# Attention's output weights multiplied into the joining weights beside the first scan; the joining product reads attention's result itself

## The chip, the cores and the metric

The kernel is one program on one core of a Trainium2 chip, in fp32 throughout. The metric is the device time of one execution in microseconds (us), and the number that counts is the median of several. A core has five engines that run their own instruction streams and meet through semaphores: TensorE (PE, matrix products; its weight loads are shown apart as PEld), VectorE (DVE), ScalarE (ACT), GpSimd (POOL) and SyncE (SP, which here issues DMA transfers).

## The reference, cut to what matters

A block of two layers over 4 images of 256 channels and 32x32 = 1024 positions. The first layer mixes channels and positions, the second is a mixture of 8 experts, two for each position.

```
x = x + metaformer(layer_norm_c(x))          # below
t = tokens(x);  t = t + experts(layer_norm(t))

def metaformer(x):                           # B=4, N=1024, C=256
    xm = four state-space scans of 64 channels (128 inner, 16 states) + skip * xn
    Q  = sigmoid(conv1d(conv1d(xm)))         # gate
    R  = conv1d(conv1d(gate * xm)) + gate * xm
    xm2 = conv1d(conv1d(cat[xs, R])) + xs
    x_local  = depthwise conv1d(xm2)
    x_global = mha(xm2)                      # 8 heads; ends in  o @ outw.T + outb
    x_out = concat[x_local, x_global] @ fc_w.T + fc_b
    xi = gelu(layernorm(x_out))
    xi = depthwise 3x3 conv(ln_hw(xi))
    return layernorm(xi) @ proj_w.T + proj_b
```

Attention's last step, `o @ outw.T + outb`, is followed by nothing but the joining product: `x_global` is the second half of what `fc_w` is multiplied with. So `x_global @ fc_g.T` equals `o @ (fc_g @ outw).T + fc_g @ outb`, with `fc_g` the half of `fc_w` that belongs to it.

## The kernel before

The data lie with channels on the 128 partitions (two chunks of 128) and positions along the free axis, mostly in halves of 512. A product of the first layer (`product`, L393) is a row of 128x512 matmuls that accumulate in one tile of PSUM: one for each chunk of 128 input channels. `in_turn` (L414) makes a list of such products and lets an ACT or DVE instruction take each result out two products later.

The order of all engines' instructions is written by hand, in Python, while the program is built. Work is given as generators; each `yield k` says that its next piece comes k ticks later. `beat` (L1475) is one tick: it lets all running generators that are due emit their next piece, in the order in which they were started. Engines then run their instructions in the order in which they were emitted, so a piece that is emitted a tick earlier stands earlier in its engine's queue, and no time is fixed.

The spine is the scan (L1521 to L1556): image b is scanned in 8 parts (4 groups of channels by 2 halves of the positions) of 16 steps. After each step (`scan`, L804) comes one beat. A step takes `decay` on ACT (L686, exp), `inflow` on DVE (L695, `dBu`), the scan instruction itself on DVE (L710, `hs`), a multiply on POOL (L718) and now and then matmuls on PE: `bs` (L681, inputs spread over states), `yp` (L728, sums over states). At fixed steps of a part the projections of the next group (`up`, `zp`, `dtp`), its silu and its softplus are emitted. SP issues the spreads of dt and c over the partitions (`dts` L652, `cs` L675), and `xd` and `XL` transfers.

Beside the scan of image b runs the rest of image b−1: `convolutions` in the first half, then, after a point at which everything running is finished, `attention` (L1069) followed by `joined` (L1216), and beside these `local`, `around` (L1258; depthwise 3x3 taps on DVE) and `sent_off` (L1301) of image b−2, which waits for a flag: `joining` of image b−1, or for the last scan `attending`. The last image's own `attention`, `joined`, `around` and `sent_off` run when the scans are over, beside the expert tiles (`tiles`, L1354): for each tile 8 `h` matmul groups (L2235), gelu on ACT (L2240, `hs`), `y` products (L2248), with the next tile's rows transposed on PE (L2194) and copied by DVE (L2198, `xT`). In this tail `pace` (L1168) sets how many ticks lie between two pieces of a tile: 2 during the joining products, 1.1 during normalisation, 0.67 during the taps.

`joined(b)` does, in this order:

- four products `ao` with the output weights `aoutT_s`, two matmuls each, on attention's result `oT` (two tiles, the former `qk` buffers); ACT takes each out as `xglo` with the bias `ob` (L1227). In ticks: a piece each 2 ticks for images 0 and 2 (10 ticks in all), each tick for images 1 and 3 (6 ticks).
- for image 2 only, it waits until image 1's `sent_off` has set `projected`.
- four products `fc` with `fcT_s`, four matmuls each: chunks 0 and 1 on `xloc`, chunks 2 and 3 on `xglo`; ACT takes each out as `xc` with the bias `fcb`.
- it sets `joining`, normalises over channels (`inverse_deviation`, L1173: squares on ACT, `var` matmuls, then `root`, L387, a logarithm and an exponential on ACT as `r`, L390 and L391, and two DVE multiplies) and applies gelu on ACT.

`sent_off(b)` takes a mean by PE (`mean`, L409), subtracts it on DVE (`xi`), finds a second deviation (`fin`), makes four products `pr` with `projT_s`, and ends with the experts' routing (`dispatch`).

`later_weights` (L209) runs once, from part 1 of image 0: the list `later` holds six weights that `load` put there (`aoutT_s` first), issued on SP at one each four ticks; then follow small preparations: `obp` (L245, the bias `ob` of attention's output from the values' bias), `prp` (L257), and the centring of `fcT_s` and of its bias `fcb` (L271 to L287), so that the mean over channels that the norm after the joining product would subtract is already zero.

Of the kernel before, what the change touches and what calls it, by code (L numbers as in the profile page):

```python
# [10 lines left out]
AF = mybir.ActivationFunctionType  # L11
ALU = mybir.AluOpType
AX = mybir.AxisListType

P = 128
C = 256
NC2 = C // P
# [58 lines left out]
def network(  # L76
# [27 lines left out]
    nc = tc.nc  # L104
    shifted = sums is None
    B = x.shape[0]
# [4 lines left out]
    def ps_tile(name):  # L111

        return psum.tile([P, HALF], F32, tag="ps", name=name)
# [9 lines left out]
    def col(name, i=0, rows=slice(0, P)):  # L123
        at = _AT[name] + i
        return V[rows, at : at + 1]

    ident = cpool.tile([P, P], F32, name="ident")
# [20 lines left out]
    with tc.tile_pool(name="w_conv", bufs=1) as wp, tc.tile_pool(  # L148
# [22 lines left out]
        def load(ap, name, eng=None):  # L171
            t = wp.tile(list(ap.shape), F32, name=name)
            if eng is None:
                later.append((t, ap))
            else:
                eng.dma_start(t, ap)
            return t
# [8 lines left out]
        nc.scalar.dma_start(inzT_s, inwT[:, :, DIN : 2 * DIN])  # L186
        xpwT_s = load(xpwT, "xpwT_s", nc.scalar)
        moutT_s = load(moutT, "moutT_s", nc.gpsimd)
        aoutT_s = load(aoutT, "aoutT_s")
        projT_s = load(projT, "projT_s")  # L190
        fcT_s = load(fcT, "fcT_s")

# [11 lines left out]
        ob = wp.tile([P, NC2], F32, name="ob")  # L204
        prb = wp.tile([P, NC2], F32, name="prb")
        fcm = wp.tile([P, 2 * NC2, 1], F32, name="fcm")
        fcb = wp.tile([P, NC2], F32, name="fcb")

        def later_weights():  # L209

            nc.sync.dma_start(vb, vbias.rearrange("a (c p) -> p (a c)", p=P))
            for t in (qdwT_s, qpwT_s, qdw_b):
                nc.gpsimd.memset(t, 0.0)
            yield 1
            nc.sync.dma_start(
                qdwT_s[:, 0 : NC2 * 3 * NB], qdwT.rearrange("p c k n -> p (c k n)")
            )
            yield 1
            for i in range(4):
                nc.sync.dma_start(qpwT_s[32 * i : 32 * i + NB, :], qpwT)  # L220
                if i % 2 == 0:
                    at = _AT["qdw_b"]
                    nc.sync.dma_start(qdw_b[32 * i : 32 * i + NB, :], vecs[0:NB, at : at + 1])
                yield 1
            for t, ap in later:
                nc.sync.dma_start(t, ap)
                yield 4
            for ci in range(NC2):
                nc.sync.dma_start(
                    wqkT_s[:, ci].rearrange("p w (i x) -> p (w i) x", x=2 * HD)  # L230
                    .rearrange("p c (i x) -> p c i x", x=HD),
                    wqkT[:, ci].rearrange("p c (i x) -> p c i x", x=2 * HD)[:, :, :, 0:HD],
                )
                yield 4
            for i in range(4):
                at = _AT["qk_b"] + i // 2
                nc.sync.dma_start(
                    qk_b[ts(i, HD), :], vecs[ds(64 * (i % 2), HD), at : at + 8 : 2]
                )
                yield 1  # L240

            obp = ps_tile("obp")
            for co in range(NC2):
                for ci in range(NC2):
                    nc.tensor.matmul(  # L245
                        obp[:, co : co + 1], aoutT_s[:, ci, ts(co, P)], vb[:, ci : ci + 1],
                        start=(ci == 0), stop=(ci == NC2 - 1),
                    )
            yield 1
            nc.vector.tensor_tensor(  # L250
                ob, obp[:, 0:NC2], V[:, _AT["attn_outb"] : _AT["attn_outb"] + NC2], ALU.add
            )

            prp = ps_tile("prp")
            for co in range(NC2):
                for ci in range(NC2):
                    nc.tensor.matmul(  # L257
                        prp[:, co : co + 1], projT_s[:, ci, ts(co, P)], col("norm_b", ci),
                        start=(ci == 0), stop=(ci == NC2 - 1),
                    )  # L260
            yield 1
            nc.vector.tensor_tensor(
                prb, prp[:, 0:NC2], V[:, _AT["proj_b"] : _AT["proj_b"] + NC2], ALU.add
            )
            for ci in range(NC2):
                nc.vector.tensor_scalar(
                    projT_s[:, ci, :], projT_s[:, ci, :], col("norm_w", ci), None, ALU.mult
                )
            yield 1

            nc.vector.tensor_reduce(fcm, fcT_s, AX.X, ALU.add)  # L271
            yield 1
            nc.vector.tensor_scalar(fcm, fcm, 1.0 / C, None, ALU.mult)
            nc.vector.tensor_tensor(
                fcT_s, fcT_s, fcm.to_broadcast([P, 2 * NC2, C]), ALU.subtract
            )
            fbp = ps_tile("fbp")
            for c in range(NC2):
                nc.tensor.matmul(
                    fbp[:, 0:1], ones_mean, col("fc_b", c), start=(c == 0), stop=(c == NC2 - 1)  # L280
                )
            yield 1
            nc.vector.tensor_tensor(
                fcb, V[:, _AT["fc_b"] : _AT["fc_b"] + NC2], fbp[:, 0:1].to_broadcast([P, NC2]),
                ALU.subtract,
            )

        ones = experts.every
# [73 lines left out]
        def a8(name):  # L362
            return act8.tile([P, NC2, N], F32, tag="a8", name=name)
# [10 lines left out]
        def a2(name, rows=P):  # L374
            return act2.tile([rows, HALF], F32, tag="a2", name=name)

        def half(h):
            return ts(h, HALF)
# [14 lines left out]
        def product(name, w, co, chunks, kept=None, at=0):  # L393

            out = ps(name)
            if kept is not None:
                nc.tensor.matmul(out, ident, kept, start=True, stop=False)
            for ci, chunk in enumerate(chunks):
                nc.tensor.matmul(
                    out, w[:, at + ci, ts(co, P)], chunk, start=(ci == 0 and kept is None),  # L400
                    stop=(ci == len(chunks) - 1),
                )
            return out
# [10 lines left out]
        def in_turn(items, make, use, lag=2, every=1):  # L414

            made, lag = [], lag // every
            for at in range(len(items) + lag):
                if at >= lag:
                    use(items[at - lag], made[at - lag])
                if at < len(items):  # L420
                    made.append(make(items[at]))
                yield every

        CO_H = [(co, h) for co in range(NC2) for h in range(2)]
# [791 lines left out]
        def joined(b):  # L1216

            xloc, oT = XLOC.pop(b), OT.pop(b)
            pace(b, PACE["product"])
            xglo = a8(f"xglo_{b}")  # L1220
            T["attending", b] = True
            yield from in_turn(
                CO_H, lambda at: product(
                    f"ao_{b}_{at[0]}_{at[1]}", aoutT_s, at[0],
                    [oT[ci][:, half(at[1])] for ci in range(NC2)],
                ),
                lambda at, r: nc.scalar.activation(  # L1227
                    xglo[:, at[0], half(at[1])], r, AF.Identity, bias=ob[:, at[0] : at[0] + 1]
                ), every=2 if b in (0, B - 2) else 1,
            )  # L1230

            while b == B - 2 and not T.get(("projected", b - 1)):
                yield 1
            xc = XC[b] = a8(f"xc_{b}")
            both = (xloc, xglo)
            yield from in_turn(
                CO_H, lambda at: product(
                    f"fc_{b}_{at[0]}_{at[1]}", fcT_s, at[0],
                    [both[ci // 2][:, ci % 2, half(at[1])] for ci in range(4)],
                ),  # L1240
                lambda at, r: nc.scalar.activation(
                    xc[:, at[0], half(at[1])], r, AF.Identity, bias=fcb[:, at[0] : at[0] + 1]
                ), lag=(4, 4, 2, 2)[b], every=(4, 2, 2, 1)[b],
            )

            T["joining", b] = True
            pace(b, PACE["norm"])
            yield from inverse_deviation(f"lgn_{b}", xc, b == B - 1)
            for c in range(NC2):
                nc.scalar.activation(  # L1250
                    xc[:, c, :], xc[:, c, :], AF.Gelu, bias=col("lgn_b", c), scale=col("lgn_w", c)
                )
            loaded[0] = None
            if b < B - 1:
                log_exp()
            yield 2
# [259 lines left out]
        with tc.manual_schedule(engines=ALL):  # L1516
# [4 lines left out]
            for b in range(B):  # L1521
                for p in range(PARTS):
                    at = b * PARTS + p
                    stop = b > 0 and p == PARTS // 2 - 1 or at == len(parts) - 1
# [883 lines left out]
```

## Time and profile before

| | us |
|---|---|
| runs | 2222.41, 2226.15, 2234.33 |
| median | 2226.15 |
| the profiled execution | 2211.61 |
| its span (first to last instruction) | 2209.9 |
| mean TensorE clock granted, of full | 0.953 |
| first and last `ao` matmul start | 548.2, 1721.1 |
| first and last scan instruction on DVE start | 55.5, 1461.9 |

The profile is of one execution, a little faster than the runs. All durations in the text come from it. In a row of a table of groups stand the line, the engine, the operation, what it writes and reads with the sizes, and how often; after the first bar the busy time and the mean of one instruction, after the second the idle time of the engine just ahead of these instructions and what ended it. Releasers are inferred from semaphores; where an instruction waits for two things, the later one is named. An fp32 matmul appears as two records, so 16 products of two matmuls are 64 records. Ends of matmuls are modelled and overlap the next one's start, so a matmul's cost in a full PE queue is read from the distance between starts.

### The profile page before, as it was taken

The numbers are of one execution on the slowest core, as the hardware profiler recorded it, in microseconds if no ns is written. First come the engines' busy times: TensorE is split into PE (matmuls) and PEld (weight loads), VectorE is DVE, ScalarE is ACT, GpSimd is POOL, SyncE is SP. The second block draws the span as 40 slices with busy tenths as digits, with TensorE's granted clock in tenths as the row PEclk, the third lists the DMA queues.
The fourth block names the chain that finished last, engine by engine and source line by source line (L and its number), as shares of the span: only waits on it lengthen the run. The fifth ranks groups of instructions, "written<-read, shape, count | busy, mean of one in ns | idle before, by whom it ended". The sixth has DMA issues, their size and how long they took to land. (4 is left out here: it accounts for less than half of the span.)

```text
span 2209.9 us, 28348 instructions
## 1 busy us (share of the span) xinstructions
PE 1971.1 (89%) x8766; PEld 881.5 (40%) x8766; DVE 1532.8 (69%) x2231; ACT 1230.8 (56%) x2302; POOL 1047.0 (47%) x930
## 2 busy tenths in 40 slices
PE   6877878999988999987889999778999999999995
PEld 2112112322212332322123223225643678888884
DVE  3989998858998978898898877985365265221211
ACT  4665657678777667775656766624167433222221
POOL 0787887712888730675985025752140022422221
PEclk8898999999999999998999999889999999999997
DMA  3665553401544421243643033344230166966655
GB/s 94 146 161 129 125 126 87 111 15 63 121 120 103 104 49 39 69 108 89 168 102 92 1 91 83 104 153 143 87 103 1 46 203 176 265 182 191 177 157 165
DMA packets 157090, 251.44 MB, mean 114 GB/s; under 512 B 34740, under 2 KB 101332, under 8 KB 156664
## 3 DMA queue, kind: packets, MB, share of 16 engines
q1 hardware_dynamic: 136560, 223.47, 37.1%
q0 software_dynamic: 12720, 17.32, 3.9%
q10 hardware_dynamic: 7640, 8.65, 1.2%
q8 instruction: 74, 1.21, 0.2%
q14 instruction: 96, 0.79, 0.1%
HBM read 137.22 MB, written 36.62 MB: 79 GB/s over the span
## 5 line engine op out<-in xcount | busy, mean ns | idle before, releaser
L718 POOL TENSOR_TENSOR dA<-hs,cs 128x512 f32<-128x512 f32 x512 | 680.2, 1338 | 388.6 <-DVE hs L710 312.9
L689 ACT ACTIVATE dA<-dts,A 128x512 f32<-128x512 f32 x512 | 359.0, 718 | 160.2 <-DMA dts<-dt 83.4
L2275 POOL DMA_INDIRECT Y<-ys,dest x68 | 109.1, 1605 | 515.7 <-DVE ys L2267 509.0
L728 PE MATMUL yp<-dA,quads 128*32 128x512 f32 x1024 | 261.6, 639 | 62.2 <-POOL dA L718 49.3
L1098 ACT ACTIVATE e<-st 128x512 f32<-128x512 f32 x512 | 263.8, 604 | 95.1 <-PE st L1088 85.0
L699 DVE TENSOR_TENSOR dBu<-dts,bs 128x512 f32<-128x512 f32 x384 | 260.2, 678 | 53.9 <-PE bs L681 13.0
L2240 ACT ACTIVATE hs<-h,b 128x256 f32<-128x256 f32 (+1 forms) x256 | 110.6, 477 | 332.8 <-PE h L2235 230.6
L2248 PE MATMUL y<-w,hs 128*128 128x256 f32 (+1 forms) x1088 | 243.6, 382 | 2.5 <-ACT hs L2240 2.5
L710 DVE TENSOR_TENSOR_SCAN hs<-dA,last,dBu 128x512 f32<-128x512 f32 x192 | 243.7, 1269 | 1.8 <-POOL xm L921 1.4
L2235 PE MATMUL h<-xT,w 128*128 128x256 f32 (+1 forms) x1024 | 238.3, 389 | 4.0 <-DVE xT L2198 4.0
L710 DVE TENSOR_TENSOR_SCAN hs<-dA,dBu 128x512 f32<-128x512 f32 x192 | 232.0, 1209 | 10.2 <-PE av L1108 5.1
L1144 DVE TENSOR_TENSOR e<-e,e 128x512 f32<-128x512 f32 x256 | 170.0, 725 | 75.6 <-ACT e L1098 39.5
L2235 PEld LDWEIGHTS h<-xT,w 128*128 128x128 f32 x1024 | 194.9, 191 | 49.6 <-issue 12.0
L2248 PEld LDWEIGHTS y<-w,hs 128*128 128x128 f32 (+1 forms) x1088 | 197.0, 188 | 39.4 <-issue 8.9
L681 PE MATMUL bs<-u,xpwT_s 128*32 128x512 f32 x1024 | 160.2, 657 | 40.4 <-DVE hs L710 16.3
L2198 DVE COPY xT<-xp 128x512 f32<-128x512 f32 (+1 forms) x36 | 23.2, 645 | 236.1 <-PE xp L2194 235.8
L1088 PE MATMUL st<-qk 32*128 32x512 f32 x1024 | 175.7, 640 | 1.9 <-DVE hs L710 1.9
L728 PEld LDWEIGHTS yp<-dA,quads 128*32 128x32 f32 x1024 | 48.3, 114 | 253.9 <-POOL dA L718 152.7
L1134 PE MATMUL av<-e,v 128*32 128x512 f32 x1024 | 139.5, 608 | 0.0
L1088 PEld LDWEIGHTS st<-qk 32*128 32x128 f32 x1024 | 60.1, 183 | 116.8 <-issue 86.2
L1108 PE MATMUL av<-e,every 128*32 128x512 f32 x512 | 87.6, 601 | 3.9 <-DVE e L1144 3.9
L699 DVE TENSOR_TENSOR bs<-dts,bs 128x512 f32<-128x512 f32 x128 | 86.2, 674 | 2.1 <-DMA dts<-dt 2.1
(330 smaller groups left out, 2716.5 us busy)
## 6 DMA issues: line engine op xcount, KB each, us to landing
dts<-dt SPq DMA_DIRECT2D x512, 128.0 KB, 2.4
w<-in_W_dram SPq DMA_DIRECT2D x124, 512.0 KB, 4.2
cs<-cd SPq DMA_DIRECT2D x512, 64.0 KB, 2.1
xs<-XS SPq DMA_DIRECT2D x32, 260.0 KB, 3.7
xd<-xn SPq DMA_DIRECT2D x64, 128.0 KB, 2.9
xn<-in_x_dram SPq DMA_DIRECT2D x8, 512.0 KB
XL<-xl SPq DMA_DIRECT2D x8, 512.0 KB
xl<-XL SPq DMA_DIRECT2D x4, 1024.0 KB
```

Source lines behind the costliest of these rows:

```text
L681: nc.tensor.matmul(bs[r], xpwT_s[:, n, s : s + 1].to_broadcast([P, 32]), T[b, n, "u"][:, half(h)], start=True, stop=True,)
L689: nc.scalar.activation(dA, T[b, n, h, "dts", g][:, 0, :], AF.Exp, scale=A[:, g, n, q : q + 1])
L699: nc.vector.tensor_tensor(dBu, T[b, n, h, "dts", g][:, 1, :], T[b, n, h, "bs", q], ALU.mult)
L710: nc.vector.tensor_tensor_scan(hs, T[b, n, h, "dA", i], dBu, 0.0 if h == 0 else last, ALU.mult, ALU.add)
L718: nc.gpsimd.tensor_tensor(dA, hs, T[b, n, h, "cs", q], ALU.mult)
L728: nc.tensor.matmul(T[b, n, h, "yp"][ts(g, 32)], quads, T[b, n, h, "dA", q * GD + g], start=False, stop=(q == GS - 1),)
L1088: nc.tensor.matmul(sts[i], k[r, ts(kt, P)], q[r, half(h)], start=True, stop=not shifted)
L1098: nc.scalar.activation(es[i], sts[i], AF.Exp, scale=1.0 / HD**0.5)
L1134: nc.tensor.matmul(accs[0][ts(i, HD)], v8[:, kt, ts(4 * g + i, HD)], es[i], start=(kt == 0), stop=(kt == NK - 1),)
L1144: nc.vector.tensor_tensor(first[i], first[i], es[i], ALU.add)
L2235: nc.tensor.matmul(hp[:, i, :], w1(c, k0 + i), xT[:, c, :], start=(c == 0), stop=(c == NC2 - 1))
L2248: nc.tensor.matmul(yp[ts(k % parts, n), ts(t % 2, C)], hidden(k)[:, ds(t * P, n)], w2(k), start=(k < parts), stop=(k >= NHC - parts),)
```

## The change

The diff does three things.

1. `aoutT_s` is no longer one of the lasting weights. It leaves the list `later` and is loaded at the end of `later_weights` into a short-lived buffer, four ticks before its use. With the list one shorter and these four ticks added, the rest of `later_weights` stands where it stood; one `yield 1` is new at its end.
2. Four transposes turn `aoutT_s` round on PE, ACT copies the result to `aout`; four matmuls of 256 columns (`joint`) multiply it with the centred half of `fcT_s` that belongs to attention, and four of one column (`fob`) multiply that half with `ob`. DVE adds `fob` to `fcb`; ACT writes `joint` over that half of `fcT_s`.
3. `joined` loses the four `ao` products, their ACT evictions, the buffer `xglo` and their ticks; the `fc` products read `oT` in place of `xglo`, with as many matmuls as before.

The flag `attending` is set at the same place, just ahead of where `ao` stood. With the ticks gone, `joining` comes ten ticks earlier for image 0 and six for images 1 and 3; image 2's wait for `projected` takes up what it lost.

```diff
--- before.py
+++ after.py
@@ -186,7 +186,6 @@
         nc.scalar.dma_start(inzT_s, inwT[:, :, DIN : 2 * DIN])
         xpwT_s = load(xpwT, "xpwT_s", nc.scalar)
         moutT_s = load(moutT, "moutT_s", nc.gpsimd)
-        aoutT_s = load(aoutT, "aoutT_s")
         projT_s = load(projT, "projT_s")
         fcT_s = load(fcT, "fcT_s")
 
@@ -239,6 +238,9 @@
                 )
                 yield 1
 
+            aoutT_s = a2("aoutT_s").rearrange("p (c x) -> p c x", c=NC2)
+            nc.sync.dma_start(aoutT_s, aoutT)
+            yield 4
             obp = ps_tile("obp")
             for co in range(NC2):
                 for ci in range(NC2):
@@ -246,10 +248,18 @@
                         obp[:, co : co + 1], aoutT_s[:, ci, ts(co, P)], vb[:, ci : ci + 1],
                         start=(ci == 0), stop=(ci == NC2 - 1),
                     )
+            turned = ps_tile("aout_turned")
+            for m in range(NC2):
+                for ci in range(NC2):
+                    nc.tensor.transpose(
+                        turned[:, ds(m * C + ci * P, P)], aoutT_s[:, ci, ts(m, P)], ident
+                    )
             yield 1
             nc.vector.tensor_tensor(
                 ob, obp[:, 0:NC2], V[:, _AT["attn_outb"] : _AT["attn_outb"] + NC2], ALU.add
             )
+            aout = a2("aout")
+            nc.scalar.copy(aout, turned)
 
             prp = ps_tile("prp")
             for co in range(NC2):
@@ -283,6 +293,25 @@
             nc.vector.tensor_tensor(
                 fcb, V[:, _AT["fc_b"] : _AT["fc_b"] + NC2], fbp[:, 0:1].to_broadcast([P, NC2]),
                 ALU.subtract,
+            )
+
+            joint, fob = ps_tile("joint"), ps_tile("fob")
+            for ci in range(NC2):
+                for m in range(NC2):
+                    nc.tensor.matmul(
+                        joint[:, ts(ci, C)], aout[:, ds(m * C + ci * P, P)],
+                        fcT_s[:, NC2 + m, :], start=(m == 0), stop=(m == NC2 - 1),
+                    )
+            for co in range(NC2):
+                for m in range(NC2):
+                    nc.tensor.matmul(
+                        fob[:, co : co + 1], fcT_s[:, NC2 + m, ts(co, P)], ob[:, m : m + 1],
+                        start=(m == 0), stop=(m == NC2 - 1),
+                    )
+            yield 1
+            nc.vector.tensor_tensor(fcb, fcb, fob[:, 0:NC2], ALU.add)
+            nc.scalar.copy(
+                fcT_s[:, NC2 : 2 * NC2, :].rearrange("p c x -> p (c x)"), joint
             )
 
         ones = experts.every
@@ -1217,26 +1246,15 @@
 
             xloc, oT = XLOC.pop(b), OT.pop(b)
             pace(b, PACE["product"])
-            xglo = a8(f"xglo_{b}")
             T["attending", b] = True
-            yield from in_turn(
-                CO_H, lambda at: product(
-                    f"ao_{b}_{at[0]}_{at[1]}", aoutT_s, at[0],
-                    [oT[ci][:, half(at[1])] for ci in range(NC2)],
-                ),
-                lambda at, r: nc.scalar.activation(
-                    xglo[:, at[0], half(at[1])], r, AF.Identity, bias=ob[:, at[0] : at[0] + 1]
-                ), every=2 if b in (0, B - 2) else 1,
-            )
-
             while b == B - 2 and not T.get(("projected", b - 1)):
                 yield 1
             xc = XC[b] = a8(f"xc_{b}")
-            both = (xloc, xglo)
+            both = [xloc[:, ci, :] for ci in range(NC2)] + oT
             yield from in_turn(
                 CO_H, lambda at: product(
                     f"fc_{b}_{at[0]}_{at[1]}", fcT_s, at[0],
-                    [both[ci // 2][:, ci % 2, half(at[1])] for ci in range(4)],
+                    [v[:, half(at[1])] for v in both],
                 ),
                 lambda at, r: nc.scalar.activation(
                     xc[:, at[0], half(at[1])], r, AF.Identity, bias=fcb[:, at[0] : at[0] + 1]
```

## The prediction

> **What bounds the kernel now.** I read the page's busy shares first, then its slices, then busy times by stage, and last the waits of the engine that each stage depends on.
>
> ```profile
> PE 1971.1 (89%) x8766; PEld 881.5 (40%) x8766; DVE 1532.8 (69%) x2231; ACT 1230.8 (56%) x2302; POOL 1047.0 (47%) x930
> PE   6877878999988999987889999778999999999995
> DVE  3989998858998978898898877985365265221211
> ```
>
> PE leads overall, but the slices (55.2 us each) show two regimes: through the scans (slices 1 to 26) DVE stands at 8 or 9 about as often as PE, and in the last nine slices PE is at 9 but for the very end and DVE at 1 to 6. So a PE microsecond has a different price in each place where the removed product ran. Those places are in the table of busy times by stretch (stretch, length, then busy time of PE, PEld, DVE, ACT, POOL with counts, granted clock, DMA share, GB/s):
>
> ```profile
> 545.00:572.00 27.00, 26.43 (x107) 8.78 (x104) 26.83 (x33) 19.27 (x41) 20.33 (x17) 1.00 0.44 103
> 909.00:946.00 37.00, 36.18 (x132) 13.57 (x136) 32.77 (x37) 27.25 (x55) 32.62 (x24) 1.00 0.43 115
> 1309.00:1333.00 24.00, 23.43 (x77) 8.47 (x75) 21.29 (x28) 14.09 (x33) 15.13 (x12) 1.00 0.32 73
> 1711.00:1749.50 38.50, 38.50 (x125) 23.30 (x125) 4.08 (x12) 13.06 (x24) 0.13 (x1) 1.00 0.13 43
> 1768.00:1882.00 114.00, 105.84 (x488) 85.48 (x487) 69.43 (x212) 35.26 (x69) 27.63 (x33) 1.00 0.67 192
> 1882.00:2170.00 288.00, 288.00 (x1359) 242.68 (x1358) 54.26 (x181) 68.63 (x156) 80.39 (x87) 1.00 0.67 184
> ```
>
> The first four are `joined` of images 0 to 3. In image 0 DVE is busy 26.83 of 27 us: PE is hidden. In image 1 PE has 36.18 of 37 and DVE lacks 4.2. In image 2 PE has 23.43 of 24 and DVE lacks 2.7. In the tail PE is full for 38.5 us and again for the 288 us before the end; between them it lacks some 8.
>
> The product itself in the table of groups (busy, mean ns | idle before), and in the timeline of the tail:
>
> ```profile
> L399 PE MATMUL ao<-qk,aoutT_s 128*128 128x512 f32 x64 | 30.0, 599 | 2.2 <-DVE hs L710 1.1 <-DVE sums L1120 1.1
> L1227 ACT ACTIVATE xglo<-ao,ob 128x512 f32<-128x512 f32 x16 | 10.7, 685 | 11.4 <-PE ao L399 11.4
> ```
>
> ```profile
> 1712.96 3.60 PE L399 MATMUL ao<-qk,aoutT_s 128*128 128x512 f32 x8
> 1716.40 1.89 PE L2235 MATMUL h<-xT,w 128*128 128x256 f32 x8
> 1718.12 3.60 PE L399 MATMUL ao<-qk,aoutT_s 128*128 128x512 f32 x8
> 1721.56 3.62 PE L2235 MATMUL h<-xT,w 128*128 128x256 f32 x16
> ```
>
> From 1712.96 to the next start at 1716.40 eight records take 3.44 us, so one takes 0.43 us: the mean of 599 ns overlaps its neighbours. 64 records are 27.5 us of PE, 6.86 for each image; ACT loses 10.7.
>
> What waits, from the waits answers of DVE in 1309 to 1345 and of PE in 1749 to 1882 (us, times, longest):
>
> ```profile
> DVE xi L1213 <- ACT r_fin L391: 3.9, 1, 3.9
> DVE dBu L699 <- ACT xglo L1227: 1.4, 1, 1.4
> DVE hs L710 <- ACT xglo L1227: 1.3, 1, 1.3
> PE h L2235 <- DVE xT L2198: 4.0, 2, 2.2
> PE y L2248 <- ACT hs L2240: 2.5, 3, 1.7
> PE pr L399 <- DVE xi L1213: 1.7, 2, 1.2
> PE mean L409 <- DVE xi L1295: 1.2, 1, 1.2
> ```
>
> In image 2 the removed eviction itself is named as the last releaser; in the tail the gaps of PE belong to DVE's taps and transposes' copies.
>
> **What the Trainium skill says.** "FP8 and Floating Point Precision", TensorE Precision Notes: true fp32 makes four passes through the array; the trace shows a 128x512 fp32 matmul as two records, 0.86 us together. "TensorE: Matmul & The Clock Gate", Architectural detail: ACT and DVE are strictly in order, and PE only pulls weight loads ahead. The trace agrees: DVE stood 1.4 and 1.3 us for evictions queued behind `ao`. The same page, Part 1, describes a clock gate that follows PE's activity: the windows view grants 0.62 in 170 to 190, and eight `bs` records take 1.93 us there. "ScalarE: Activation LUTs", on the table load, gives about 1283 ns for it; the trace's mean for such loads is 1283 as well.
>
> **The change, part by part.**
>
> *The fold, once.* Added beside image 0's scan: 4 transposes, 4 joint matmuls (8 records), 4 one-column `fob` matmuls (8 records), two ACT copies and one DVE add. The load of `aoutT` moves on SP from 92.9 us to about 152.5, right behind the first half of an `XL` load; it waits there for a POOL multiply that is early, and behind it stand the spread loads of c and dt, which the timeline shows in time, so I cost it 0. `obp` and `prp`, eight one-column records each, take 1.87 and 1.85 us at this clock (0.23 each). The transposes, a quarter of a 512-column record, are about 0.15 each at full clock and 0.3 at this one; they delay `prp`, and with it DVE's `prb`, by about 0.7. The joint product's 8 records of 256 columns take 1.7 at full clock, 3.4 at half; `fob`, at the 0.23 of `obp`, about 1.8. These 3.3 to 5.7 us start at the fcT subtraction's end at 182.7, and DVE reaches the `fcb` add one beat, about 3.6 us, later: a stall of 0 to 2.1. DVE is busy 19.97 of 20 us there, so each stall is lost. Sum +2.3; bounds 0 (all hidden) and +5 (both stalls full and the later tick costs one more).
>
> *Image 0: −0.8.* DVE covers the product. Only one DVE idle of 0.82 at 611.9 hangs on PE. Bounds 0 and −2.
>
> *Image 1: −4.1.* The 6.86 us go from a stretch where PE is the fuller engine. DVE's idles in it are 2.55 at 921.8 (released by ACT's `r`, which sits behind the product), 0.77 and 0.76: together 4.08; with these gone DVE is full, so no more can come. But six ticks fall out, and `joining` and with it `sent_off(0)` come six beats earlier against the scan (I counted 412 to 406, in program order). That block holds 11.2 us of DVE idles between 979 and 1014; in which direction they go is open. Bounds −9 (half of them fall away too) and +5 (half of them again).
>
> *Image 2: −2.9.* 1.28 and 1.39 go with the evictions. The 3.87 at 1341.6 hangs on `r_fin`: its variance matmul at 1331.4 stands behind the last `ao` at 1329.7, then come two table loads. That chain and the scan move forward together, so it mostly stays; I give it 0.2. Image 2's waiting loop makes up the removed ticks, so the order after it is unchanged. Bounds 0 and −5.5 (half a further stall of the chain shortened: 2.8).
>
> *The tail: −6.7.* 6.86 of PE go out of 38.5 full us. I replayed the after-order with the trace's durations. The normalisation's variance then waits about 2.6 for the squares, since the expert matmuls that filled this are shorter in number; `h` of tile 8 waits 4.5 instead of 1.8, because DVE now has four more taps ahead of that tile's transposed copy; `mean_3` waits 3.9 instead of 1.2, `pr` 2.3 instead of 1.7. Against that, two stalls of `y` behind table loads (0.57 and 1.72) and one of `h` behind a copy (2.16) go, as tiles and joined part no longer meet. The lead is 4.4 at tile 6, 2.6 at tile 9, 4.6 at tile 12 and 6.7 from tile 13 on; from 1882 on PE is 100% busy and carries it to the end. The final wait for the last expert rows comes after it in the same order. Bounds −4 (the stalls at tile 8 and `mean` stay as replayed, those behind the table loads too) and −9 (the new stalls don't come).
>
> Sum: 2.3 − 0.8 − 4.1 − 2.9 − 6.7 = −12.2. The profiled execution took 2211.6 us (span 2209.9), so 2199.4 by its measure. It lies 14.5 under the median of the runs shown, 2226.15; applied to this, 2213.95, said as 2214. A measurement here tells 0.5%, or 11.1 us, from no change: the border is at 2215.0, close to my sum.
>
> **Rivals.**
>
> A. *PE's time pays in full in images 1 and 2 and the tail*: 3 × 6.86 = 20.6, less 2.3: −18.3, 2207.9. For it: PE is 98% busy in both `joined` stretches, and a shorter PE queue ahead of `bs`, `up` and `yp` also removes idles further on that the waits answers put down to PE (4.67 at 1004). Against it: DVE lacks just 4.1 and 2.7 us in them.
>
> B. *Only the tail pays*: the scan's DVE idles move to the next late thing (`r_fin`, `silu` with its table load). −6.7 + 2.3 = −4.4, 2221.8. For it: after the removed product the same chain of root, table load and normalisation follows. Against it: two of the idles name the removed eviction.
>
> C. *The moved block costs more than the product saved.* In image 1 `sent_off(0)` meets the scan six beats earlier, so that its table loads and its `XR` waits fall beside step events fixed to the part's beats (silu, the next part's projections), and the 11.2 us of idles of 979 to 1014 double; the fold costs its +5. 11.2 + 5 − 6.7 − 2.9 = +6.6, 2232.8. It decides once image 1 loses more than 4.6 us with the fold at its bound (6.7 + 2.9 − 5). For it: that stretch shows POOL `dt` 1.3, ACT `xm` 2.3, PE `bs` 4.7 as releasers, an order that met badly. Against it: nothing is added there, and a bad meeting is as likely to be undone.
>
> That the change doesn't do what it says is excluded by the code: 16 products and 16 evictions are gone and 4 once-only matmuls replace them.
>
> **How the numbers follow.** Main sum 0.43, A 0.33, B 0.13, C 0.11. The main case has its own range of −8 to −16 (2210 to 2218), and 58% of it lies below 2215. Faster by over 0.5%: 0.58 × 0.43 + 0.95 × 0.33 = 0.56. Slower by over 0.5% (above 2237.3): nearly half of C and a tenth of B, 0.06. The rest, 0.38, is within it. Range 2203 to 2228: low end in A's lower part, high end above B; it leaves out about a tenth of A's own spread, most of C and a sliver of B.
>
> **What would show it.** Right: DVE without the two `xglo` idles at about 1328 and 1332; the stretch of `joined(1)` shorter by about 4; a lead at the end of the scan of about 5.5, and 12 at the end; `h` of tile 8 and `mean_3` waiting longer than before, `y` no longer for `hs`. Wrong: a DVE stall over 2.5 us at `fcb`'s second add; idles in `sent_off(0)` that grow past 11.2 (C); a lead before the tail already above 9 (A) or near −2 (B); or a lead that is lost in the experts by stalls of `h` behind `xT` over 5 us.

## The result, and the profile after

The changed kernel took 2215.61 us (median of 9 runs, 2207.31 to 2222.07) against 2226.56 us (9 runs, 2221.80 to 2236.28): a ratio of 0.9934, interval 0.9912 to 0.9955. Applied to 2226.56 that is 14.7 us less, somewhere between 10.0 and 19.6. The forecast was 12.2 less, 2214.0.

The first profile of the changed kernel misleads: its span is 2215.0 us, longer than the 2209.9 of the kernel before. Both kernels were therefore profiled once more, and these two agree with the runs: 2212.0 before, 2196.9 changed, 15.1 us apart. Where the first profile of the changed kernel lost its time is shown below, under "Both kernels once more".

From the second profile of the changed kernel, the page's busy shares:

```profile
PE 1960.0 (89%) x8722; PEld 875.3 (40%) x8722; DVE 1534.8 (70%) x2232; ACT 1223.6 (56%) x2288; POOL 1048.0 (48%) x930
```

PE has 44 instructions fewer (64 records of `ao` out, 20 of the fold in), ACT 14 fewer. PE's share is the same 89%: between the second profiles its busy time fell by 13.5 us (from 1973.5) and the span by 15.1.

What matters is where. I cut both traces at instructions that both kernels have: the first scan instruction on DVE of a part (for the end of image 1's stretch and both ends of image 2's the scan instruction just before it), and in the tail the first `h` matmul of an expert tile. Busy times by stretch, with columns as before. The kernel before, second profile:

```profile
148.84:189.10 40.26, 27.81 (x107) 8.57 (x102) 36.87 (x44) 22.13 (x40) 32.69 (x25) 0.73 0.56 138
538.89:661.15 122.26, 107.13 (x418) 28.74 (x416) 119.95 (x139) 88.83 (x163) 95.84 (x75) 1.00 0.47 115
897.52:1059.28 161.76, 136.00 (x512) 44.62 (x510) 140.35 (x197) 106.07 (x197) 105.61 (x84) 0.92 0.38 98
1202.16:1346.12 143.96, 136.58 (x779) 39.30 (x778) 113.96 (x149) 104.35 (x204) 26.80 (x20) 0.97 0.20 53
1713.77:1884.35 170.58, 160.12 (x686) 122.10 (x685) 81.08 (x238) 61.87 (x113) 30.93 (x36) 1.00 0.50 143
```

The changed kernel, second profile:

```profile
145.22:187.97 42.75, 28.78 (x115) 12.79 (x108) 37.29 (x45) 19.22 (x36) 33.45 (x25) 0.79 0.52 132
536.29:659.78 123.49, 108.23 (x402) 27.13 (x400) 120.15 (x138) 86.76 (x159) 96.09 (x75) 0.97 0.47 115
899.51:1056.51 157.00, 133.08 (x498) 42.77 (x494) 139.27 (x197) 104.07 (x193) 109.82 (x89) 0.92 0.40 103
1202.87:1341.23 138.36, 130.64 (x763) 36.34 (x762) 113.74 (x148) 102.61 (x200) 26.82 (x20) 0.97 0.20 54
1707.01:1869.71 162.70, 155.17 (x669) 120.89 (x669) 81.62 (x238) 59.27 (x109) 31.61 (x38) 0.98 0.50 147
```

In order: the fold's place (image 0's scan, from its fourth to its fifth part), images 0, 1 and 2's joined part with what runs beside it, and the tail from tile 5 to tile 13. Lengths change by +2.5, +1.2, −4.8, −5.6 and −7.9. DVE's busy time is the same in every stretch to within about 1 us. In the scans, what left is time in which DVE stood; in the tail it is 5.0 us of PE's busy time and 2.9 in which PE stood.

From tile 13 on the two kernels run alike, as forecast: 61.55 us for the next four tiles and 213.24 for the fourteen after them, in both second profiles.

### The profile page after: what moved, and what is told of

It reads as the page before. It is cut to its first block, busy times and chain, and to the rows that moved or that the text cites. A ratio compares the mean times of both kernels' runs of the same rounds, so it can differ in the third digit from the quotient of the medians.

```text
span 2215.0 us, 28220 instructions
## 1 busy us (share of the span) xinstructions
PE 1975.0 (89%) x8722; PEld 879.7 (40%) x8722; DVE 1534.4 (69%) x2232; ACT 1222.4 (55%) x2288; POOL 1047.5 (47%) x930
## 5 line engine op out<-in xcount | busy, mean ns | idle before, releaser
L718 ACT ACTIVATE dA<-dts,A 128x512 f32<-128x512 f32 x512 | 358.8, 718 | 143.5 <-DMA dts<-dt 72.4
L757 PE MATMUL yp<-dA,quads 128*32 128x512 f32 x1024 | 272.2, 632 | 71.2 <-POOL dA L747 60.9
L1117 PE MATMUL st<-qk 32*128 32x512 f32 x1024 | 182.0, 645 | 7.0 <-ACT e L1127 3.0
```

The source lines that it names most:

```text
L718: nc.scalar.activation(dA, T[b, n, h, "dts", g][:, 0, :], AF.Exp, scale=A[:, g, n, q : q + 1])
L757: nc.tensor.matmul(T[b, n, h, "yp"][ts(g, 32)], quads, T[b, n, h, "dA", q * GD + g], start=False, stop=(q == GS - 1),)
L1117: nc.tensor.matmul(sts[i], k[r, ts(kt, P)], q[r, half(h)], start=True, stop=not shifted)
```

## The experiments

The table holds the stretches of all kernels, in us, worked out from the same instructions. "Joined 0" and so on are the stretches of those images, "tail" is tile 5 to 13. Ratios are against runs of the kernel before that were taken beside each experiment. The stretches don't cover the whole kernel; what lies between image 1's and image 2's is added under ticks_kept.

| kernel | fold | joined 0 | joined 1 | joined 2 | tail | ratio, interval |
|---|---|---|---|---|---|---|
| before, first profile | 40.64 | 123.35 | 162.08 | 143.96 | 170.55 | |
| again_before | 40.26 | 122.26 | 161.76 | 143.96 | 170.57 | |
| fold_alone | 42.35 | 123.61 | 161.66 | 144.15 | 170.58 | 0.9998, 0.9982 to 1.0013 |
| tail_alone | 41.93 | 125.54 | 162.09 | 143.89 | 162.69 | 0.9979, 0.9967 to 0.9991 |
| product_kept | 42.53 | 125.06 | 162.30 | 142.21 | 170.62 | 1.0003, 0.9991 to 1.0015 |
| changed, first profile | 41.71 | 124.96 | 158.42 | 138.93 | 163.99 | 0.9934, 0.9912 to 0.9955 |
| again_after | 42.75 | 123.49 | 157.00 | 138.37 | 162.70 | |
| ticks_kept | 42.60 | 123.93 | 158.03 | 139.26 | 163.76 | 0.9932, 0.9911 to 0.9953 |
| fold_later | 40.51 | 124.94 | 158.53 | 138.64 | 162.78 | 0.9919, 0.9887 to 0.9951 |
| tail_two_ticks | 40.64 | 123.49 | 157.01 | 138.60 | 164.45 | 0.9917, 0.9890 to 0.9945 |
| tail_three_ticks | 40.63 | 123.48 | 155.57 | 137.65 | 166.43 | 0.9924, 0.9898 to 0.9949 |
| tail_four_ticks | 40.76 | 125.20 | 161.07 | 137.65 | 164.04 | 0.9931, 0.9905 to 0.9956 |

### Both kernels once more

again_before, no edit:

> The kernel before once more, for a second profile. The changed kernel's profile lost 15 us between its 128th and 160th tile matmul (1597 to 1722 us, attention of the last image, untouched by the change), where ACT waited 7.5 us with no releaser in the program. Theory 'chance': such stalls fall in any execution, so this profile differs from the first by several us in some stretch and its span lies anywhere from 2208 to 2230. Rival 'fixed by the program': all starts of scan parts and tiles agree with the first profile within 1 us, span 2208 to 2212.

again_after, no edit:

> The changed kernel once more, for a second profile. Theory 'chance': the stretch from the 128th tile matmul to the 160th takes about 110 us as in the kernel before (it took 125 in the first profile), and the span is 2197 to 2205 unless another stall falls. Rival 'fixed by the program': 125 us again, with ACT's e waiting 7 us on no engine. Both: the scan's part starts as in the first profile within 1 us: image 0's joined about +1.6 to +3 against before, image 1's about -3.7, image 2's about -5.

The spans were 2212.0 and 2196.9, and the stretch from the 128th tile matmul to the 160th, that is from tile 4 to tile 5, took 109.99 and 109.98 us. In the first profile of the changed kernel it took 125.04; in all other profiles of this study it lies between 109.97 and 109.99. One of ACT's waits there, in the first profile (1620 to 1720):

```profile
ACT e L1127 <- remote: 7.9, 2, 7.5
```

"Remote" is a wait that no recorded instruction or transfer of the program ended; of the twelve profiles of this study it stands in this one alone. Theory "chance" holds: 15 us of that profile aren't the change's. PE's clock stood at half for 6.8 us twice in that stretch, from 1635 and, as the wait of 7.5 ended, from 1649. What caused ACT's wait was not found. (The span of 2212.0 fits both ranges that were given for again_before; the changed kernel's second profile decides.)

That part starts would agree within 1 us did not hold: between the two profiles of one kernel some parts differ by 3.2 us. These disagreements have a cause that shows. In the third part of image 1's scan, with image 0's convolutions beside it, where both kernels have the same instructions, three profiles give three lengths: 32.89 (before, first), 34.49 (changed, second) and 36.08 (changed, first); the fourth, again_before, has 36.14, so the two profiles of the kernel before lie 3.25 apart here. Busy times by stretch and DVE's longest wait in the three, in this order:

```profile
377.00:410.00 33.00, 30.57 (x108) 11.26 (x109) 30.37 (x35) 22.30 (x46) 25.70 (x20) 1.00 0.45 108
DVE dBu L699 <- PE bs L681: 1.6, 1, 1.6
```

```profile
376.00:411.00 35.00, 31.85 (x109) 11.22 (x107) 30.78 (x36) 22.48 (x46) 26.43 (x20) 0.95 0.44 99
DVE dBu L728 <- PE bs L710: 3.2, 1, 3.2
```

```profile
374.00:411.00 37.00, 33.59 (x107) 11.62 (x108) 31.18 (x36) 23.26 (x46) 26.69 (x20) 0.91 0.41 98
DVE dBu L728 <- PE bs L710: 4.8, 1, 4.8
```

The granted clock falls from 1.00 to 0.95 and 0.91 and the wait grows by 1.6 each time. The clock records show none, one and two periods of 3.4 us at half clock there. They begin 8 to 9 us into the part and DVE's wait ends 22.6 to 25.8 us into it, so the clock comes first.

### The fold by itself

```diff
+ fcg = wp.tile([P, NC2, C], F32, name="fcg")
+ fcb2 = wp.tile([P, NC2], F32, name="fcb2")
...
- nc.vector.tensor_tensor(fcb, fcb, fob[:, 0:NC2], ALU.add)
- nc.scalar.copy(fcT_s[:, NC2 : 2 * NC2, :]..., joint)
+ nc.vector.tensor_tensor(fcb2, fcb, fob[:, 0:NC2], ALU.add)
+ nc.scalar.copy(fcg.rearrange("p c x -> p (c x)"), joint)
```

(A cut, with a line shortened; against the changed kernel; `joined` is that of the kernel before, and `aoutT_s` stays among the lasting weights, so the moved load isn't part of this test.) This kernel, tail_alone and product_kept also lower the buffer counts `bufs` of two small statistics tiles, from 2 and 3 to 1. fold_alone has the stretches of the kernel before everywhere but in the fold's place, so these cost nothing that shows.

> The kernel before with the fold computed beside image 0's scan into tiles of its own, which nothing reads; the joined part is as before. My sum: +2.3 us (0 to +5), ratio 1.001. Rival from the first pair of profiles: the fold is hidden, part 5 of image 0 starts within 0.7 us of before, ratio 1.000. A third, that the fold itself brings some of the gain by shifting the scan, would give 0.997 or less.

The stretch took 42.35 us, 1.9 more than the mean of the two profiles before (40.45), and the six kernels with the fold as written average 42.3. A wait of DVE accounts for it:

```profile
DVE fcb L313 <- PE fob L308: 1.8, 1, 1.8
```

My sum's +2.3 is near; the whole run doesn't resolve it (0.9998). Nothing after the stretch moves: the fold brings nothing by itself.

fold_later takes the wait away:

```diff
-            yield 1
+            yield 2
             nc.vector.tensor_tensor(fcb, fcb, fob[:, 0:NC2], ALU.add)
```

> The changed kernel with one more tick ahead of DVE's second add to fcb, so that PE's fob is done before DVE comes to it. Theory 'the fold costs what DVE stands for at that add (1.8 us)': the wait is gone, part 3 of image 0 takes about 40.5 us instead of 42.2, ratio 0.9926 against 0.9934. Rival 'the fold costs through PE's queue (bs behind joint and fob)': the wait moves to dBu behind bs and the part stays at 42.

DVE's waits in its fold stretch:

```profile
DVE hs L739 <- POOL dA L747: 2.6, 1, 2.6
DVE xn L558 <- POOL xl L556: 0.7, 1, 0.7
DVE prb L272 <- PE prp L267: 0.2, 1, 0.2
```

No `fcb` among them, and the stretch is 40.51, the length before. The three kernels built on fold_later have 40.63 to 40.76. So the fold's matmuls and the moved load cost nothing; the add that asked for them too early cost 1.8. The version is faster than the kernel before (0.9919); against the change itself so small a gain is too little for the intervals.

### Is it the PE time, or the earlier ticks?

ticks_kept leaves the product out and its ticks in:

```diff
             T["attending", b] = True
+            yield 10 if b in (0, B - 2) else 6
```

> The changed kernel with the removed product's ticks left in place as an empty wait (10, 6, 10, 6), so that joining and all that follows it come at the same ticks as before. Theory 'the removed PE time is the gain': ratio 0.993 to 0.995 as with the change, image 1's part starts about 4 us earlier without the swing of +7 and -8 in its parts 5 to 7, image 0's about -1 instead of +1.6 to +3. Rival 'the earlier ticks are the gain in image 1': image 1 gains under 1 us, ratio 0.996 or more.

The gains in images 1 and 2 stay (joined 1 158.03, joined 2 139.26), with nothing moved; image 0 did not come out at −1 (123.93). In the tail all of the product's time is there and no more: the lead stands at 6.87 us at tile 6 and between 6.81 and 6.82 from tile 7 on, one image's 6.86 of PE, with PE's waits as before and full clock. Counted from the start of joined 1's stretch, the scan's parts in the changed kernel come first up to 4.2 us later and at its end 4.8 earlier than before (second profiles); here they come 2.2, 3.2 and 3.7 earlier, one after the other. The earlier ticks are not the gain.

They have a price that the table doesn't show. From the end of joined 1 to the start of joined 2, where no edit adds or removes an instruction, the six kernels that keep the ticks of images 0 to 2 take 142.88 to 143.03 us, ticks_kept among them (143.01). The six without take 144.98 to 147.82, 2.9 more on the mean. Most of it lies in the third part of image 3's scan: 32.90 in all of the first six, 34.49 to 36.11 in the others, at a granted clock of 1.00 and of 0.95 to 0.91. So the earlier ticks give back 2.0 to 4.8 of what image 1 gained. Why the periods at half clock fall into that part without the ticks was not tested.

product_kept is the reverse: folded weights for all images, and the 16 products still issued in their ticks, with nothing to take them out (a cut, against the kernel before):

```diff
-                lambda at, r: nc.scalar.activation(xglo[...], r, AF.Identity, bias=ob[...])
+                lambda at, r: None
```

> As the changed kernel in what it computes, with folded weights for all images, but the 16 products with the output weights are still issued on PE, in their old ticks, and nothing takes their results out: PE's work is back, ACT's 16 evictions and the wait of fc for them are not. Theory 'PE's time is the gain': image 1's stretch (parts 4 of scan 2 to 0 of scan 3) is back at 161 to 162 us, image 2's joined gives at most half of its 5.3, the tail nothing: ratio 0.999 to 1.001. Rival 'ACT's evictions and the wait behind them are the gain': image 1 still -3 or more, image 2 still -4 or more, ratio 0.994 to 0.996.

Ratio 1.0003. The fold's 1.9 us are in it. Joined 1 is back at 162.30 and the tail at 170.62, within 0.6 and 0.1 of what they were. Joined 2 keeps 1.8 of its 5.6, and even that may not be the evictions: product_kept shows one period of 3.4 us at half clock in this stretch, where the kernel before and the changed one show two of 6.8. So PE's time is the gain, and the evictions by themselves account for 1.8 at most.

### The tail by itself

```diff
+        FOLDED = (3,)
...
+            folded = b in FOLDED
...
+            glo = oT if folded else [xglo[:, ci, :] for ci in range(NC2)]
```

> Image 3 alone reads the folded weights (kept in tiles of their own); images 0 to 2 keep the product with the output weights. My sum with the sizes now measured: fold +1.9, nothing in the scans, tail -7.5 (342.1 us from the 128th to the 544th tile matmul before, 334.2 in the second profile of the changed kernel): -5.6 us, ratio 0.9975. Rival 'the tail's gain comes from what the scans hand over': the stretch stays at 340 or more, ratio 0.999 to 1.001.

The tail took 162.69, the same as in the whole change, with scans as before: it doesn't depend on what the scans hand over. The ratio, 0.9979, fits −7.9 + 1.9 = −6.0 (0.9973).

PE's waits in the tail, of the changed kernel (second profile, 1707 to 1870):

```profile
PE xp L2212 <- DMA xs<-XS: 4.2, 1, 4.2
PE var_lgn L438 <- ACT sq_lgn L1209: 1.6, 1, 1.6
PE pr L428 <- DVE xi L1242: 0.9, 1, 0.9
PE places L1861 <- ACT hs L2258: 0.5, 1, 0.5
PE h L2253 <- DVE xT L2216: 0.2, 1, 0.2
PE mean L438 <- DVE xi L1313: 0.2, 1, 0.2
```

They add up to 7.6 us. Before, PE stood 10.5 in this stretch (170.58 less 160.12 busy). So 2.9 of the 7.9 are fewer waits: 2.5 of `y` and nearly all of `h` went, 4.2 of `xp` and 1.6 of `var` came. The other 5.0 are busy time, less than the product's 6.86. The clock granted is 0.98 in place of 1.00: it falls to half for 6.8 us at 1767.64, right behind the wait of 4.2. ticks_kept has neither this wait nor a drop of the clock, and is 1.1 us longer (163.76): that is what the missing ticks bring in the tail, net. tail_four_ticks, tail_two_ticks and tail_three_ticks put some of image 3's ticks back into fold_later, to be rid of the 4.2 (a cut of the first; the other two have 2 and 3):

```diff
+            if b == B - 1:
+                yield 4
```

> fold_later with four of image 3's six removed ticks put back as an empty wait. In the changed kernel tile 8's transposes wait 4.2 us for their rows, whose load stands behind a table that DVE counts after the taps. Theory 'order of DVE': with the table ahead of more taps the wait falls to 2 or less and the tail stretch to 332 us (342.1 before, 334.2 as changed): ratio 0.992. Rival 'the old meeting of tiles and joined part returns': y waits for hs again (2.6) and the stretch is 335, as with all ticks kept (335.3): ratio 0.9935.

> fold_later with two of image 3's six ticks put back. With four, tiles 6 and 7 (192nd to 256th tile matmul) took 30.7 us instead of 35.7, since the table stood ahead of more taps, but tiles 10 to 12 took 57.1 instead of 49.7. Theory 'the two effects can be had apart': 160th to 416th in 160 us or less (162.8 in fold_later, 164.0 with four), ratio 0.991. Rival 'one pays for the other at every setting': 162 to 165, ratio 0.992 to 0.993.

> The same with three ticks put back. Theory 'the two effects can be had apart': 160th to 416th tile matmul in 160 us or less, ratio 0.991. Rival 'one pays for the other at every setting': 162 to 165, ratio 0.992 to 0.993.

Tiles 6 and 7 fell to 30.7 us each time (35.7 in fold_later), and the tiles behind them took it back: the tail took 164.04 with four ticks, 164.45 with two and 166.43 with three, against 162.78. With four, `y` waits for `hs` again (2.3), as the rival said. The theory of two separate effects falls: one wait pays for the other, or costs more, at every setting tried. Three ticks came out longer than the 162 to 165 of the rival as well.

## Why the prediction was right, point by point

| step | forecast | measured |
|---|---|---|
| fold | +2.3 | +1.9 |
| image 0 | −0.8 | +0.5 |
| image 1 | −4.1 | −3.9 |
| between image 1 and image 2 | 0 | +2.9 |
| image 2 | −2.9 | −5.5 |
| tail | −6.7 | −7.9 |
| sum | −12.2 | −12.0 |

Measured are means of the table's rows: with the product in the first four rows (for the fold, the first two against the six with the fold as written), without it in the last seven; for the stretch between, the six kernels with the ticks against the six without; for the tail, again_before and again_after. That the two sums are so close is luck: image 2 and the tail paid 3.8 more than forecast, and image 0 and the stretch behind image 1 took 4.2 back. The runs say −14.7 (−10.0 to −19.6) and the two second profiles lie 15.1 apart; the difference to −12.0 isn't located. It is within what unchanged stretches scatter: from the start to the fold's place the twelve profiles take 143.5 to 151.7.

**The fold** was right in size and kind: a stall of DVE at the second add, forecast at 0 to 2.1, was 1.8. The other part, 0.7 at `prb`, was 0.2. The forecast's own terms, 1.7 to 3.4 and 1.8, add up to 3.5 to 5.2 us of PE and not to 3.3 to 5.7, so the stall should have read 0 to 1.6; 1.6 and 0.7 make its 2.3. `joint` and `fob` took 5.3 together, and the four transposes came 0.23 apart. (What the prediction calls 4 once-only matmuls, against the 16 products, are these four transposes and four calls each for `joint` and `fob`.) The moved load cost nothing, as forecast.

**Image 0**: rows with the product run from 122.26 to 125.54, those without from 123.48 to 125.20. The product was hidden under DVE, as said; neither the 0.8 nor the +0.5 of the means can be told from zero in that scatter.

**Image 1** was right in its own stretch, and ticks_kept and product_kept show the reason. Of DVE's waits there, in again_before:

```profile
DVE dBu L699 <- PE bs L681: 6.2, 3, 4.7
DVE dBu L699 <- ACT r L390: 2.5, 1, 2.5
```

The forecast's 4.08 are the 2.5 behind `r` and the two short ones behind `bs`. In ticks_kept exactly these are gone: nothing waits for `r`, and `bs` has one wait of 4.7 left. In product_kept they are back (2.0 for `r`, three for `bs`). In the change itself, where the block has moved, the waits are others (again_after):

```profile
DVE dBu L728 <- PE bs L710: 5.4, 1, 5.4
DVE dBu L728 <- ACT xr L1346: 3.0, 1, 3.0
```

That it ends at about the same length is partly luck. And the forecast put the effect of the earlier ticks at nothing: right behind, they cost 2.9 on the mean, so that the change keeps about 1.0 of image 1's gain and ticks_kept all of it. The bounds of this term don't follow from its own reasons: half of 11.2 on either side of −4.1 gives −9.7 and +1.5, not −9 and +5. One row is out of line, tail_four_ticks with 161.07; it lost 2.5 in the part beside attention, which none of the edits touches.

**Image 2** is the term that was mis-sized. I wrote that the `r_fin` chain "mostly stays" and gave it 0.2; it gave about 2.6. The timeline of PE, ACT and DVE at the end of that chain, before (second profile):

```profile
1334.21 3.60 PE L409 MATMUL var_fin<-sq_fin,ones_mean 128*128 128x512 f32 x8
1336.13 0.69 ACT L390 ACTIVATE r_fin<-var_fin,eps 128x512 f32<-128x512 f32 x1 [1.03 <-PE var_fin L409]
1344.38 1.23 DVE L1213 TENSOR_TENSOR xi<-xi,r_fin 128x1024 f32<-128x1024 f32 x1 [3.87 <-ACT r_fin L391]
```

and changed:

```profile
1329.08 1.88 PE L438 MATMUL var_fin<-sq_fin,ones_mean 128*128 128x512 f32 x4
1331.24 0.68 ACT L419 ACTIVATE r_fin<-var_fin,eps 128x512 f32<-128x512 f32 x1
1339.49 1.23 DVE L1242 TENSOR_TENSOR xi<-xi,r_fin 128x1024 f32<-128x1024 f32 x1 [1.26 <-ACT r_fin L420]
```

From the first `r_fin` to DVE's `xi` lie 8.25 us in both. The stretch starts at 1202.16 and 1202.87, so `r_fin` comes 5.6 earlier in it, and DVE's `xi` and the stretch's end with it. DVE stands at `xi` in both cases, so the chain from `r_fin` on set the end, not the sum of idles ahead of it. Before, ACT stood 1.03 for `var_fin`, which stood behind the last `ao` on PE. With `ao` gone, `var_fin`'s first half is done when ACT comes to `r_fin`, behind a copy that follows the scan: PE no longer starts the chain, the scan does, and DVE with fewer stops brings it forward. DVE's wait there shrank from 3.87 to 1.26, which with the 1.28 and 1.39 of the evictions is 5.3. I had the right line and asked how much of the idle would go, rather than what starts the chain. product_kept agrees: with the product on PE again, `xi` waits 5.1 for `r_fin`.

**The tail** was right in size, and ticks_kept shows the product's 6.86 in it; its inner course was only partly right. The waits as forecast don't even give the forecast's lead: 6.86 less the added 2.6, 2.7, 2.7 and 0.6, plus the 0.57, 1.72 and 2.16 that go, is 2.7 and not 6.7. That the size came out is in this respect luck: most of the added waits didn't come. Of the new waits, one of about 4.5 at tile 8 came (4.2), though as a late load of the tile's rows and not as a late copy (the DMA queue waits 23.7 us for `taken`, the table that DVE works out); `var` took 1.6 rather than 2.6, and those forecast for `mean` (3.9) and `pr` (2.3) were 0.2 and 0.9. That the lead dips from tile 8 on and is whole again from tile 13 was as forecast; it dipped further, to 0.65 at tile 9 (forecast 2.6).

**The rivals.** B falls: images 1 and 2 pay 9.4 in their own stretches, 6.5 with what lies between. C falls: image 1 with the stretch behind it doesn't lose, let alone 4.6; but its mechanism was there, a block that comes earlier and costs, with the 2.9. A isn't excluded by the runs alone, since −18.3 lies within −10.0 to −19.6. It is by the stretches: image 2 with 5.5 and the tail with 7.9 paid most of a product or more, image 1 with 3.9 didn't. The lead ahead of the tail was 6.8 between the second profiles, where the main case had about 5.5 and A above 9.

## What to carry to other kernels

Where a stretch ends with an engine standing, follow back what it stands for to the point where that chain starts: work removed ahead of the start moves the whole chain. Adding up the idles in between came out too small in image 2, while in image 1, where no such chain ends the stretch, it came out right. Removing waiting steps together with work is a second change: here the steps taken out cost 2.9 us behind image 1 and brought 1.1 in the tail, so test the two apart. Weights that are folded once beside other work cost only as much as the first instruction that asks for them too soon; ask one step later. A single profile can be off by more than the change: cut two at instructions that both kernels have, and look first whether a stretch that the change doesn't touch differs.

## What was not expected of the hardware

The Trainium skill, "TensorE: Matmul & The Clock Gate", section "What's actually happening", says that the clock gate looks at PE's activity in a window of about 3.4 us that runs freely, so that the phase differs from run to run. The clock records agree: apart from the first record of each trace, every stretch at half or full clock lasts a multiple of 3.41 us. Not expected was what this does to a long kernel. In the stretch shown, PE stands 2.1 us at the same place, 5.0 us into the part, in all four profiles of the two kernels. In one of them no drop follows, in one a period of 3.4 us and in two a double one, and each period adds 1.6 us: 32.89, 34.49, 36.08 and 36.14. The third part of image 2's scan shows the same steps (32.90 and 36.13 in the two profiles of the changed kernel). In the third part of image 3's scan they aren't chance: there the kernels with and without the ticks differ throughout, as said under ticks_kept. The twelve profiles hold between 200 and 237 us at half clock.

Once in the twelve profiles ACT waited 7.5 us for nothing that the trace names (and once more 3.5 in the same execution); with the two drops of the clock around it that stretch lost 15 us.
